# Two graph layers on one core: transposes of the parked batches, and their loads, spread over two steps

## The chip, the cores and the metric

The kernel runs on one core of a Trainium2 chip. The metric is device time in microseconds (us), lower is better. Engines: PE (TensorE, matrix products), DVE (VectorE, elementwise work and 32x32 transposes), ACT (ScalarE, sigmoid, tanh, ReLU and copies out of PSUM), POOL (GpSimd, a few small powers), and SP (SyncE), whose queue issues every DMA of this kernel. Each engine takes its instructions strictly in the order in which they were written.

## The reference

There are 16 batches of 1024 nodes with 128 features, and one dense 1024 x 1024 matrix `adj`. All is float32.

```
h = relu(layernorm(x));  x1 = x + (adj @ (h @ W) + bias)          # layer 0
h = relu(layernorm(x1))                                           # layer 1
repeat 5 times:                                                   # a gated graph step
    m = adj @ h                                                   # in_matrix and out_matrix are both adj
    z = sigmoid(m @ (W3a+W3b) + h @ U3 + biases)
    r = sigmoid(m @ (W4a+W4b) + h @ U3 + biases)
    v = tanh(m @ (W5a+W5b) + (r*h) @ U5 + biases)
    h = (1-z)*h + z*v
out = x1 + h
```

## The kernel before

**Steps.** The batches are worked in four quads of four: quad 0 is batches 0 to 3, quad 1 is 4 to 7, and so on. A step is written (quad, n), n from 0 to 4, and has two stretches. In the *aggregation* `adj @ h` is computed for the quad, with Strassen's scheme at two levels (`aggregate`, 49 small products of four PE records each, about 0.86 us a product). In the *gates* (`gates`, 34.3 us on PE) the small weights are applied, first for pair A (batches 0 and 1 of the quad), then for pair B (batches 2 and 3). A pair has four units (batch, half); its phases are r (four units), z (four) and v (four). Two quads are in work at once, and their steps alternate: (0,0), (1,0), (0,1), [layer 0 of quad 2], (1,1), (0,2), (1,2), (0,3), (1,3), [layer 0 of quad 3], (0,4), (1,4), (2,0), (3,0), (2,1), and so on to (3,4).

**Right operands.** Of the 49 products, 40 take their right operand from `ring` (12 slots). Two operands make one load of 512 KB (`ring<-rd`), issued when a slot has been used; 20 loads for an aggregation. Five of them are issued in the gates before, or at their end (`GATE_LOADS`).

**Left operands** come from `nat`, four loads for each batch (`nat<-fn`, `nat<-ft`), and are added up by DVE and copied by ACT into `big` and `little`, partly in the gates before (`GATE_PLACES`). Among the first of an aggregation are `big[2]` at place 1 and the sums behind it.

**Places.** All side work is hung on places by `put(k, piece)`: place k, a number, is reached after k products of the aggregation; a place with a name is in the gates: `Ar0` comes after the r phase's first unit of pair A, `Az1` after the z phase's second, `Br0` and `Bz1` the same in pair B. At a place the pieces come in the order in which they were put. A place sets where an instruction stands in its engine's queue, SP's included.

**State.** The hidden state stands transposed in `hT_all` (two sets of four batches; quads 0 and 2 use set 0, quads 1 and 3 set 1). After a batch's new state is made, DVE turns it into squares (`sq`, line 669), and SP stores these (`fn<-sq`).

**Norms and parked batches.** In the gates of a step named in `NORMS` DVE takes the statistics of two batches (line 332: four and four `bn_stats` around Ar3 and Az1 for the first, Br3 and Bz1 for the second). In the aggregation of the next step DVE makes their `nmr` (line 349, place 10), and ACT makes the normalized, rectified batch (line 362, from place 11 on). It is *parked*: four stores `ft<-hb` at place 22 for the first and 36 for the second, each followed by a store of x1 (`x1d<-xt`). Before a quad's first step each of its parked batches is loaded (`sqt<-ft`, 512 KB, function `transposing`) and turned into `hT_all` by two DVE transposes of 128 x 512 (line 701).

**Buffers that matter.** `flip` has three buffers for `sq`, `sqt`, `hb`, `ha` and `ho` together. `hv`, which ACT's tanh writes (line 837) and DVE's three update operations use up (lines 238, 839, 241), has three, so that a pair's fourth tanh writes the buffer of its first. An aggregation's PSUM banks are emptied by ACT copies (line 523), and the product that goes on in a bank waits for the copy before.

**Where the turns stand before.** `TRANSPOSED` names the step and the quad: quad 1 in (1,0), quad 2 in (1,4), quad 3 in (3,0). All four loads of a quad stand at places 8, 18, 28 and 38 of that step's aggregation, their turns at 17, 27, 37 and 47. Quad 0's turns are in layer 0 and not touched.

Of the kernel before, what the change touches and what calls it, by code (L numbers as in the profile page):

```python
# [87 lines left out]
    (0, 2): ((12, 26), (13, "Ar1")),  # L88
    (1, 2): ((14, 26), (15, "Ar1")),
}  # L90
TRANSPOSED = {(1, 0): 1, (1, 4): 2, (3, 0): 3}
OUTPUTS = {(3, 0): 0, (2, 1): 1, (3, 1): 2, (2, 2): 3, (3, 2): 4, (2, 3): 5, (3, 3): 6, (2, 4): 7}
UNITS = ((0, 0), (0, 1), (1, 0), (1, 1))

# [2 lines left out]
def tile_two_gnn_layers(  # L97
# [17 lines left out]
    Q = 4  # L115
# [12 lines left out]
    def dma(out, in_):  # L128
        pin(nc.sync.dma_start(out=out, in_=in_))
# [4 lines left out]
    def x_tile(b):  # L134
        return pre.tile([P, NC, D], F32, tag="xt", name=f"xt_{b}")

    def load_x(b, xt=None, parts=((0, NC),)):
        xt = xt if xt is not None else x_tile(b)
        for cs in parts:
            cs = slice(*cs)  # L140
            dma(xt[:, cs], by_slots(x[b])[:, cs])
        return xt
# [14 lines left out]
    hT_all = const.tile([P, 2, Q, N], F32, tag="hT", name="hT_all")  # L157
# [274 lines left out]
    def early_pieces(n):  # L432
        bigs, smalls = left_pieces(n)
        return bigs[0] + smalls[0] + bigs[1] + bigs[3] + smalls[1][:2]

    def period(i):
        return 2 + 7 * i
# [217 lines left out]
    def flip_tile(nm):  # L655
        return flip.tile([P, NSQ, NC, SQ], F32, tag="sq", name=nm)

    def squares_of_half(sq, g):
        return sq[:, :, bass.ts(g, CH), :].rearrange("p k j e -> p j k e")

    def transposed_half(hT, g):
        return hT[:, bass.ts(g, HALF)].rearrange("p (j k e) -> p j k e", j=CH, k=NSQ)
# [28 lines left out]
    def transposing(b, hT):  # L691

        box = {}

        def load():
            box["sq"] = flip_tile(f"sqt_{b}")
            dma(box["sq"].rearrange("p k j e -> p (k j e)"), parked[b][0])

        def turn():
            for g in range(NH):  # L700
                pin(nc.vector.transpose(transposed_half(hT, g), squares_of_half(box["sq"], g)))

        return load, turn
# [4 lines left out]
    def put(k, *pieces):  # L708
        fixed.setdefault(k, []).extend(pieces)
# [56 lines left out]
    def put_statistics(kind, first):  # L766

        rest = []
        for n, b in enumerate((first, first + 1)):
            box = {}  # L770

            def begin(b=b, box=box):
                box["n"] = Norm(xts[b], None, f"{kind}{b}")
                box["n"].statistics(range(CH))

            def relu(k, b=b, box=box):
                def run():
                    if k == 0:
                        box["n"].dst = flip_tile(f"h{kind}_{b}")
                    box["n"].relu(range(2 * k, 2 * k + 2))  # L780

                return run

            def done(b=b, box=box):
                (keep if kind == "a" else layer_1_input)(b, box["n"].dst)

            key = "AB"[n]
            put(f"{key}r3", begin)
            put(f"{key}z1", lambda box=box: box["n"].statistics(range(CH, NC)))
            put(f"{key}z3", lambda box=box: box["n"].scales(EVERY))  # L790
            rest.append((10, lambda box=box: box["n"].shift(EVERY)))
            rest += [(11 + 13 * n + 3 * k, relu(k)) for k in range(CH)]
            rest.append((22 + 14 * n, done))
            if kind == "a":
                rest.append((("Ar0", "Br0")[n], lambda b=b: bias(b)))
        return rest
# [181 lines left out]
    def loads_of_next(source, places):  # L978

        for k, at in enumerate(places):  # L980
            put(at, lambda k=k: natural_from(source[k], nat[:, k]))

    def step(i, loads_at=(period(4), period(5), "Ar0", "Ar2"), early_places=GATE_PLACES):
        st = state[i]
        quad, n = st["quad"], st["step"]
        nm = f"{quad}_{n}"
        hT = [hT_all[:, i, k] for k in range(Q)]
        last = n == STEPS - 1
        final = last and quad == quads - 1
        other = state[1 - i]  # L990
        me = (quad, n)
        for k, piece in relus.pop("next", ()):
            put(k, piece)
        for b, k in LOADS.get(me, ()):
            put(k, lambda b=b: xts.update({b: load_x(b)}))
        if me in TRANSPOSED:
            q = TRANSPOSED[me]
            for k in range(Q):
                load, turn_it = transposing(q * Q + k, hT_all[:, q % 2, k])
                put(8 + 10 * k, load)  # L1000
                put(17 + 10 * k, turn_it)
        if me in OUTPUTS:
            for k, piece in zip((16, 34, 38), outputs[OUTPUTS[me]]):
                put(k, piece)
        block = BLOCKS.get(me)

        source = h0_of(block) if block else other["blocks"]
        if final:
            st["x1"] = []

            def load_x1(k):
                x1 = x_tile(f"1_{quad * Q + k}")
                dma(x1, x1s[quad * Q + k])
                st["x1"].append(x1)

            for k, places in enumerate(((None, 10, 13), (12, 24, 27), (26, 39, 41), (37, "R10", "R11"))):
                for piece, at in zip(outputs[(quad - 1) * Q + k], places):
                    if at is not None:
                        put(at, piece)
            for k, at in enumerate(("R00", "R01", "Z01", "V10")):  # L1020
                put(at, lambda k=k: load_x1(k))
        if source is not None:
            loads_of_next(source, loads_at)
        aggregate(nm, place)
        if me in NORMS:
            relus["next"] = put_statistics(*NORMS[me])
        if source is not None:
            for k, piece in zip(early_places, early_pieces(made[0])):
                put(k, piece)
        stored, ready = {}, {}  # L1030

        def turn(first):
            def run(k):
                k += first
                stored[k] = Later(lambda n: ready[k][n])

                def squares():
                    store, ready[k] = squares_to_dram(hT[k], f"{nm}_{k}")
                    if k >= Q - 2:
                        put({Q - 2: 4, Q - 1: 9}[k], store)  # L1040
                    else:
                        store()

                if k == Q - 1:
                    put(3, squares)
                else:
                    squares()

            return run

        if last:
            outputs.update({quad * Q + k: output(quad * Q + k, Later(lambda n, k=k: ready[k][n])) for k in range(Q)})
            if quad == quads - 2:
                put("Bz1", outputs[quad * Q][0])
        if final:
            last_gates(quad, hT, st["x1"])
            st["quad"], st["blocks"] = None, None
            return
        for a, key in enumerate("AB"):
            pair = slice(2 * a, 2 * a + 2)  # L1060
            gates(
                [mT[:, 2 * a + k] for k in range(2)],
                hT[pair],
                f"{nm}{key}",
                key,
                turn(2 * a),
            )
        st["step"] += 1
        st["blocks"] = [stored[k] for k in range(Q)]
        if last:  # L1070
            begin(i, quad + 2)
        if block:
            loads_of_next(other["blocks"], (period(3) + 4, period(4) + 4, period(5) + 2, period(6)))
            pieces = early_pieces(made[0] + 1)
            for k, piece in zip(BLOCK_PLACES, pieces):
                put(k, piece)
            aggregate(f"a{block}", place, gates_follow=False)
            for k in range(Q):
                for g in range(NH):
                    po(block * Q + k, g)  # L1080
                    if 2 * k + g in (1, 2, 6, 7):
                        pieces[{1: 6, 2: 7, 6: 8, 7: 9}[2 * k + g]]()
            for piece in pieces[10:]:
                piece()
# [4 lines left out]
    def begin(i, quad):  # L1089

        if quad >= quads:
            state[i] = {"quad": None, "blocks": None}
            return
        state[i] = {"quad": quad, "step": 0, "blocks": parked_of(quad)}
# [13 lines left out]
    def h0_of(quad):  # L1108
        return Later(lambda k: h0_blocks[quad * Q + k])
# [108 lines left out]
    for k in range(Q):  # L1218
        b = Q + k
# [56 lines left out]
```

## Time and profile before

| | us |
|---|---|
| median of 3 runs | 1774.37 (1773.52 to 1776.88) |
| profiled execution | 1779.16 |
| its span | 1777.4 |
| PE busy / DVE busy / ACT busy | 1761.9 / 1372.8 / 903.7 |
| gates of (0,0) | 170 to 204 |
| aggregation, gates of (1,0) | 204 to 247, 247 to 281 |
| aggregation, gates of (1,4) | 920 to 963, 963 to 997 |
| aggregation, gates of (2,0) | 997 to 1040, 1040 to 1074 |
| aggregation, gates of (3,0) | 1074 to 1119, 1119 to 1153 |

The span runs from the first to the last of the program's own instructions; around it lie 1.8 us. In rows of instruction groups the numbers are busy time, mean of one in ns, idle time of the engine before them. In rows of the timeline they are start and duration in us, and in brackets the engine's idle time before and what ended it. In lists of waits they are total, times, longest. Names of tiles are shown without the quad: `r_0A` is the r of step 0, pair A, of any quad.

### The profile page before, as it was taken

To read this page: it belongs to the slowest core of one execution; us is meant where nothing else is said; L and a number is where in the kernel's file an instruction comes from. 1 tells how busy PE (TensorE), PEld (TensorE's weight loads), DVE (VectorE), ACT (ScalarE), POOL (GpSimd) and SP (SyncE) were. 2 spreads that over 40 slices of the span, in tenths; PEclk is the share of its full clock that TensorE was granted. 3 is DMA by queue.
4 is the path that set the end of the run, shared out by engine and by line. 5 is a ranking of instruction groups with operands and counts; after the bars stand their busy time and mean duration, and the time that the engine had idled before them with its cause. 6 is when DMAs were issued, how large, how long until landed. Compare 5 with 4: busy or idle time off the path is not lost.

```text
span 1777.4 us, 21433 instructions
## 1 busy us (share of the span) xinstructions
PE 1761.9 (99%) x6438; PEld 1200.4 (68%) x6438; DVE 1372.8 (77%) x2806; ACT 903.7 (51%) x1974; POOL 59.3 (3%) x41
## 2 busy tenths in 40 slices
PE   9999999999999999999999999999999999999998
PEld 3557667588586675858857667585776857667584
DVE  6778988776879687877687968777687777867787
ACT  5246556544555555554455554545445454445544
POOL 3101000000000000000000000000000000000000
PEclk9999999999999999999999999999999999999999
DMA  7489786688395856749839578694866849476794
GB/s 257 158 310 308 235 250 215 176 253 252 123 310 181 267 198 192 241 133 282 263 132 312 185 222 255 168 292 157 250 205 198 253 131 307 153 234 219 195 291 171
DMA packets 169970, 396.88 MB, mean 223 GB/s; under 512 B 18560, under 2 KB 88064, under 8 KB 169856
## 3 DMA queue, kind: packets, MB, share of 16 engines
q1 hardware_dynamic: 169856, 395.52, 70.8%
q8 instruction: 52, 0.85, 0.2%
q14 instruction: 62, 0.51, 0.1%
HBM read 314.44 MB, written 81.00 MB: 222 GB/s over the span
## 4 chain that ended last, share of the span: by engine, by line
PE 89%; DMA 5%; DVE 4%; ACT 1%; POOL 1%; issue 0%; SPq 0%; DVEq 0%; POOLq 0%
PE a L504 25%; PE c L504 12%; PE b L504 6%; PE a_a L504 3%; DMA ring<-rd 3%; PE pr_3B L808 2%; PE pr_1B L808 2%; PE pr_0B L808 2%; PE pr_2B L808 2%; PE pr_2A L808 2%; PE pr_1A L808 2%; PE pr_0A L808 2%; PE pr_3A L808 2%; PE a_a L620 2%; PE pv_0B L808 2%; PE pv_3B L808 2%
## 5 line engine op out<-in xcount | busy, mean ns | idle before, releaser
L504 PE MATMUL a<-ring,big 128*128 128x256 f32 x1120 | 288.3, 380 | 4.4 <-DMA ring<-rd 3.7
L523 ACT COPY Z<-a 128x256 f32<-128x256 f32 x480 | 177.2, 371 | 198.9 <-PE a L504 198.6
L241 DVE TENSOR_TENSOR Z<-Z,taps 128x512 f32<-128x512 f32 (+1 forms) x264 | 144.5, 554 | 167.2 <-ACT taps L523 166.9
L504 PE MATMUL c<-ring,little 128*128 128x256 f32 x960 | 246.6, 379 | 1.2 <-DMA ring<-rd 1.1
L504 PEld LDWEIGHTS a<-ring,big 128*128 128x128 f32 x1120 | 211.7, 190 | 43.5 <-issue 10.5
L241 DVE TENSOR_TENSOR mT<-mT,Z 128x1024 f32<-128x1024 f32 x154 | 188.3, 1223 | 27.4 <-ACT Z L523 22.3
L504 PEld LDWEIGHTS c<-ring,little 128*128 128x128 f32 x960 | 182.0, 190 | 26.9 <-ACT Z L523 1.5
L523 ACT COPY taps<-c 128x256 f32<-128x256 f32 x280 | 103.6, 370 | 117.2 <-PE c L504 112.5
L504 PE MATMUL b<-ring,big 128*128 128x256 f32 x560 | 143.8, 379 | 1.0 <-DMA ring<-rd 1.0
L504 PE MATMUL a<-resident,little 128*128 128x256 f32 x560 | 143.8, 379 | 0.0
L504 PE MATMUL a<-ring,little 128*128 128x256 f32 x560 | 143.7, 379 | 0.0
L504 PEld LDWEIGHTS b<-ring,big 128*128 128x128 f32 x560 | 106.3, 190 | 15.8 <-DMA ring<-rd 1.4
L504 PEld LDWEIGHTS a<-resident,little 128*128 128x128 f32 x560 | 106.3, 190 | 14.7 <-ACT Z L523 0.3
L504 PEld LDWEIGHTS a<-ring,little 128*128 128x128 f32 x560 | 106.4, 190 | 14.5
L669 DVE STREAM_TRANSPOSE sq<-hT_all 128x512 f32<-128x512 f32 x152 | 98.6, 687 | 0.0
L523 ACT COPY taps<-b 128x256 f32<-128x256 f32 x140 | 52.0, 372 | 56.7 <-PE b L504 55.8
L401 ACT COPY big<-nat 128x512 f32<-128x512 f32 x132 | 80.6, 614 | 0.1
L238 DVE TENSOR_TENSOR little<-little,big 128x256 f32<-128x256 f32 x154 | 65.4, 425 | 6.7
L238 DVE TENSOR_TENSOR little<-big 128x256 f32<-128x256 f32 x154 | 64.3, 418 | 0.0
L238 DVE TENSOR_TENSOR little<-big,little 128x256 f32<-128x256 f32 x154 | 64.2, 417 | 0.0
L241 DVE TENSOR_TENSOR little<-big 128x256 f32<-128x256 f32 x154 | 64.0, 416 | 0.2
L523 ACT COPY mT<-a 128x256 f32<-128x256 f32 x80 | 29.8, 372 | 48.1 <-PE a L504 48.0
(282 smaller groups left out, 2912.6 us busy)
## 6 DMA issues: line engine op xcount, KB each, us to landing
ring<-rd SPq DMA_DIRECT2D x440, 512.0 KB, 6.3
fn<-sq SPq DMA_DIRECT2D x76, 512.0 KB, 3.7
nat<-fn SPq DMA_DIRECT2D x256, 128.0 KB, 6.6
x1d<-xt SPq DMA_DIRECT2D x16, 512.0 KB, 5.9
sqt<-ft SPq DMA_DIRECT2D x16, 512.0 KB, 6.8
xt<-x1d SPq DMA_DIRECT2D x16, 512.0 KB, 7.6
xt<-in_x_dram SPq DMA_DIRECT2D x15, 512.0 KB, 6.2
out_dram<-xt SPq DMA_DIRECT2D x14, 512.0 KB, 7.9
```

The costliest lines, as they stand in the source:

```text
L238: pin(nc.vector.tensor_sub(o, a, b))
L241: pin(nc.vector.tensor_add(o, a, b))
L401: return [lambda i=i: pin(nc.scalar.copy(made_of(k, i), part(a, b, i))) for i in range(2)]
L504: nc.tensor.matmul(bank, l, right[:, c, :], start=opens and c == 0, stop=c == SB - 1, skip_group_check=True,)
L523: pin(nc.scalar.copy(to, bank))
L620: nc.tensor.matmul(bank, left[:, c, :], right[c // SB][:, c % SB], start=p in (1, 2, 5) and c == 0, stop=c == CH - 1, skip_group_check=True,)
L669: pin(nc.vector.transpose(squares_of_half(sq, g), transposed_half(hT, g)))
L808: nc.tensor.matmul(bank, w_sb[:, w, :], moving, start=start, stop=stop, skip_group_check=True)
```

## The change

`TRANSPOSED` now lists single batches, each with the place of its load and of its turn. No instruction is added or removed.

```diff
-TRANSPOSED = {(1, 0): 1, (1, 4): 2, (3, 0): 3}
+TRANSPOSED = {
+    (0, 0): ((4, "Ar0", "Az1"), (5, "Br0", "Bz1")),
+    (1, 0): ((6, 8, 17), (7, 28, 34)),
+    (1, 4): ((8, 8, 17), (9, 25, 34), (10, "Ar0", "Az1"), (11, "Br0", "Bz1")),
+    (2, 0): ((12, 8, 17), (13, 25, 34), (14, "Ar0", "Az1"), (15, "Br0", "Bz1")),
+}
...
-        if me in TRANSPOSED:
-            q = TRANSPOSED[me]
-            for k in range(Q):
-                load, turn_it = transposing(q * Q + k, hT_all[:, q % 2, k])
-                put(8 + 10 * k, load)
-                put(17 + 10 * k, turn_it)
+        for b, load_at, turn_at in TRANSPOSED.get(me, ()):
+            load, turn_it = transposing(b, hT_all[:, b // Q % 2, b % Q])
+            put(load_at, load)
+            put(turn_at, turn_it)
```

Quad 1's first two batches move from the aggregation of (1,0) to the gates of (0,0), its last two stay there at places 8 and 28. Of quad 2 two stay in the aggregation of (1,4), two move into that step's gates. All of quad 3 moves from (3,0) to the step before, (2,0): two into its aggregation, two into its gates. On SP the load of batch 4 comes to stand behind the x load of batch 11 and ahead of the third and fourth group of `nat` loads; that of batch 5 behind the store of batch 1's squares; those of batches 10 and 14 behind the second group of `nat` loads; those of 11 and 15 behind the store of their step's second batch. On DVE the turn at Az1 stands among the statistics or early sums of pair A, the turn at Bz1 among those of pair B, ahead of the updates of that pair. Line numbers of the changed kernel are 5 higher behind the table, and 3 higher behind the loop.

## The prediction

> **What bounds the kernel now.** I read the page first, then the list of waits, then single stretches of the timeline.
>
> ```profile
> PE 1761.9 (99%) x6438; PEld 1200.4 (68%) x6438; DVE 1372.8 (77%) x2806; ACT 903.7 (51%) x1974; POOL 59.3 (3%) x41
> ```
>
> PE is busy for 1761.9 of 1777.4 us at a granted clock of 0.999, and the change neither adds nor removes a matmul. All that it can move is PE's idle time, 15.5 us, and new idle time. PE's waits over the whole span:
>
> ```profile
> PE a L504 <- DMA ring<-rd: 3.7, 5, 2.0
> PE c L504 <- DMA ring<-rd: 1.1, 1, 1.1
> PE b L504 <- DMA ring<-rd: 1.0, 1, 1.0
> PE a L504 <- ACT Z L523: 0.7, 3, 0.3
> ```
>
> 5.8 us go to late ring loads. Asked step by step, only two of the steps touched have any. Aggregation (3,0), 1074 to 1119 us, has the first two lines below (1.8 us); aggregation (1,4), 920 to 963, the third.
>
> ```profile
> PE c L504 <- DMA ring<-rd: 1.1, 1, 1.1
> PE a L504 <- DMA ring<-rd: 0.7, 1, 0.7
> ...
> PE a L504 <- DMA ring<-rd: 0.4, 1, 0.4
> ```
>
> The last line of the whole list, "ACT Z", is small but matters most. One of its three waits is at the head of (1,0). ACT there:
>
> ```profile
> 213.92 0.37 ACT L523 COPY taps<-c 128x256 f32<-128x256 f32 x1 [0.49 <-PE c L504]
> 215.74 0.88 ACT L362 ACTIVATE ha<-xt,nmr_a,rstd_a 128x128 f32<-128x128 f32 x2 [1.45 <-DVE nmr_a L349]
> 216.53 0.62 ACT L523 COPY Z<-a 128x256 f32<-128x256 f32 x2
> ```
>
> ACT stands behind nmr of DVE, and the bank copies behind it end at 217.15; the matmul that waits for them starts at 217.20, 0.03 us late. So in a step whose predecessor made statistics ((1,0) after (0,0), (2,0) after (1,4)), DVE has no room at all at the head of the aggregation: lateness that it carries there is PE's. And DVE carries it, since it isn't idle in the second half of such gates.
>
> **The change, part by part.** Sixteen loads (sqt, 512 KB) and sixteen double transposes stay sixteen; twelve of each are concerned. A double transpose holds DVE 1.23 us (967.77 to the next operation at 969.00).
>
> *Taken from aggregations.* (1,0) loses two of its four loads and turns, (1,4) two, (3,0) all four; (2,0) gains two. In (3,0) 4 x 512 KB leave a stretch where the DMA share is 0.96, so its 1.8 us of ring waits should go: -1.8. In (1,4) two loads leave ahead of the late one: -0.4. (1,0) and (2,0) have no ring wait to lose. Two more loads in (2,0) (share 0.87) could cost up to 2 x 1.25 us if all of it were late (1.25 us is 512 KB at the 415 GB/s of a full queue). But (1,4), with the same parking and four such loads, waits 0.4, so two cost 0 to 0.4; I take 0, as PE comes there later anyway (below). DVE's shorter aggregations gain nothing, as no PE wait names those turns.
>
> *Put into the gates of (0,0).* The load of batch 4 goes to Ar0, on SP's queue behind the last x load, and its turn to Az1. DVE and SP there now:
>
> ```profile
> 178.29 1.64 DVE L332 BATCH_NORM_STATS2 stats_a<-xt 128x6 f32<-128x128 f32 x8
> 179.84 0.62 DVE L341 BATCH_NORM_AGGREGATE mv_a<-stats_a 128x2 f32<-128x6 f32 x8
> ...
> 182.82 0.69 DVE L238 TENSOR_TENSOR hv_0A<-hv_0A,hT_all 128x512 f32<-128x512 f32 x1 [2.15 <-ACT hv_0A L837]
> ```
>
> ```profile
> 175.18 0.35 SPq L129 DMA_DIRECT2D xt<-in_x_dram  x1
> 175.88 2.88 SPq L129 DMA_DIRECT2D nat<-ft  x4
> ```
>
> The turn stands after four of the eight statistics (179.05). 2.15 us of idle follow, so it is free if the load lands by 182.82 - 1.60 (the work still to do) - 1.23 = 180.0. But SP issues it only at about 175.9, after the x load, which takes 7.6 us (lands 182.8), because the queues are full from 160 to 192 us. 512 KB at that stretch's 255 to 394 GB/s are 1.3 to 2.1 us, so it lands at 184.1 to 184.9; I take 184.4. DVE is then 4.4 us late. [...] A lone ring load at 206.14 took 3.3 us[...]; here four small loads issued at 175.9 to 178.5 took 6.5 to 7.6, and the row decides.
>
> Queued behind the turn on DVE are the updates of pair A, the squares and r*h of pair B, which PE needs at 198.21 and now has at 194.38: 4.4 us late makes PE wait about 0.6. The rest stays. At Bz1 the turn of batch 5 follows: its load goes out behind the store of batch 1's squares, about 4.2 us before it lands (the ring load at 194.25 took 4.2), just in time for DVE's place (198.95 + 4.4 against 203.0). Another 1.23:
>
> ```profile
> 201.87 0.68 DVE L238 TENSOR_TENSOR hv_0B<-hv_0B,hT_all 128x512 f32<-128x512 f32 x1
> ...
> 203.38 0.69 DVE L241 TENSOR_TENSOR hT_all<-hT_all,hv_0B 128x512 f32<-128x512 f32 x1
> ```
>
> The sum 203.38 + 0.69 + 5.6 = 209.7 frees the hv buffer (three of them) that ACT's fourth tanh, at 204.42 now, writes. ACT is in order, so the copy of the first bank, at 205.28 now, comes about 210.5, and the matmul that needs it (206.81) waits near 4; the nmr chain takes the remainder. With no room in that chain, **the whole 4.4 + 1.2 = 5.6 us reach PE**. Bounds: 1.2 (the load in time, only the Bz1 turn uncovered) to 6.2 (landing 184.9).
>
> *Put into the gates of (1,4).* They start better than now:
>
> ```profile
> 967.77 1.30 DVE L701 STREAM_TRANSPOSE hT_all<-sqt 128x512 f32<-128x512 f32 x2 [6.75 <-DMA sqt<-ft]
> ```
>
> This wait goes: the last two loads move behind it, and Ar0's load, ahead of which SP has two loads less, lands before Az1. What the gates then cost I take from (0,4), which has the same statistics and no turns: 0.69 us idle before hv of pair A, so the Az1 turn leaves 1.23 - 0.69 = 0.54. At Bz1 DVE arrives at 912.93 + 0.54 = 913.5 on that clock; the store before the load goes out at 909.29 + 0.54, the load 0.4 later, 4.2 to land: 914.4. It waits 1.0, then turns 1.23: 2.8 late at pair B's first update. Now (1,4) is there 1.96 late ((994.96 - 962.65) - (915.85 - 885.50)), because of the 6.75. Net +0.85 at the head of (2,0), which has no room. Bounds 0 (load in time) to 2.5 (both turns wholly uncovered).
>
> *Put into the gates of (2,0).* No statistics there, idle 2.99 us before pair A's update and 1.81 before B's: both turns are covered, a late landing included (about 1.4 us late at worst, and (3,0) has no nmr chain). Without that cover 1.2 each.
>
> *Ring loads in the gates* come 1.25 us later behind each moved load. They are used over 17 us after they land. Moved past on SP they cost nothing.
>
> **Sum** against the profiled span: 5.6 + 0.85 - 0.4 - 1.8 = +4.3, 1777.4 to 1781.7 us. That execution took 1779.16 in all, 4.8 more than the median 1774.37 of the plain runs; about that much of ring waits may be the profiler's own, so plain runs may lack both the -2.2 and a part of the backlog behind the +5.6. The two errors oppose each other. On the median: 1778.7.
>
> **Rivals.**
> - *The cover holds* (not slower). One mechanism: the load of batch 4 lands by 180.0. [...] Then (0,0) costs 1.2, (1,4) about 0: 1.2 - 2.2 = -1.0, 1773.4 us. It decides from a landing below about 182, where the sum falls under 3.5 us.
> - *Half cover.* It lands near 182: 2.0 + 1.2 + 0.85 - 2.2 = +1.9, 1776.3.
> - *Ring waits grow in (2,0).* Both added loads fall into a full queue: 4.3 + 2.5 = 6.8, 1781.2. Against it: the 0.4 of (1,4) with four.
> - *No effect:* all moved work is hidden, ring waits are only the profiler's: 1774.4. The idle 2.15 and 2.99 us speak for it, the ACT row at 215.74 against it.
> - *Faster:* it would take the 3.3 us of ring waits in untouched steps to go too, 1774.4 - 5.5 = 1768.9. Nothing in the profile links them.
>
> **How the numbers follow.** Main case 0.53 (own range 1777 to 1780.7, the landing's bounds), ring waits grow 0.10, half cover 0.13, cover holds 0.12, no effect 0.07, faster 0.05. A change within 0.2% (3.5 us) can't be told from none. Of the main case about a tenth lies below 1777.9, so slower is 0.48 + 0.10 + a few hundredths of half cover = 0.62; same is 0.31, faster 0.07. The range, 1773.0 to 1781.6, leaves out "faster" and the tails.
>
> **What would show it.** Right: in the gates of (0,0) a DVE transpose with about 5 us idle before it, released by the sqt load; ACT's fourth tanh of pair B released by DVE; a PE wait of some 4 us at the head of (1,0); no ring wait in (3,0). Wrong: that transpose starts by 180 us, or PE doesn't wait at the head of (1,0); or ring waits appear at the end of (2,0).

## The result and the profile after

The changed kernel takes 1780.38 us (median of 5 runs, 1778.8 to 1782.6), the kernel before 1774.33 beside it. The ratio of matched runs is 1.0026, 95% interval 1.0014 to 1.0038: slower by some 4.6 us (2.5 to 6.7). That figure comes from runs paired in time; the two medians alone lie 6.05 us apart. The prediction was +4.3 us.

The two profiled executions can't be set against each other as totals: the one of before took 1779.16 us, more than its median, and the one of after 1778.80. Only their stretches can be compared. PE's work on the page of after is what it was:

```profile
PE 1762.0 (99%) x6438; PEld 1201.8 (68%) x6438; DVE 1373.8 (77%) x2806; ACT 903.4 (51%) x1974; POOL 59.3 (3%) x41
```

PE's list of waits over the span of after (total, times, longest):

```profile
PE a L509 <- ACT mT L528: 3.1, 1, 3.1
...
PE a L509 <- ACT Z L528: 1.3, 2, 1.0
PE a L509 <- DMA ring<-rd: 1.3, 1, 1.3
```

The first line is new and is the head of aggregation (1,0). Of the second, 1.0 us is the head of (2,0). The ring waits of (1,4) and (3,0) are gone, and the one that is left lies near 600 us, in a step that the change does not touch.

**DVE in the gates of (0,0)**, timeline of after (start, duration, in brackets the idle time before and what ended it):

```profile
178.19 0.87 DVE L337 BATCH_NORM_STATS2 stats_a<-xt 128x6 f32<-128x128 f32 x4
183.77 1.31 DVE L706 STREAM_TRANSPOSE hT_all<-sqt 128x512 f32<-128x512 f32 x2 [4.71 <-DMA sqt<-ft]
...
186.48 0.68 DVE L243 TENSOR_TENSOR hv_0A<-hv_0A,hT_all 128x512 f32<-128x512 f32 x1
...
202.63 1.30 DVE L706 STREAM_TRANSPOSE hT_all<-sqt 128x512 f32<-128x512 f32 x2
...
206.75 0.68 DVE L243 TENSOR_TENSOR hv_0B<-hv_0B,hT_all 128x512 f32<-128x512 f32 x1
```

The load of batch 4 was issued at 175.3 and landed 8.4 us later. DVE waits 4.71 us for it after half of the statistics and is 3.66 us late at pair A's first update (182.82 before). The second turn needs no wait, takes its 1.2 us, and pair B's first update starts at 206.75 instead of 201.87. PE's matmuls ahead of this stretch start 0.10 us earlier than in before (the start-up of the two executions), so DVE is **4.98 us late**.

**ACT behind it**, same stretch of after:

```profile
209.04 0.69 ACT L842 ACTIVATE hv_0B<-pv_0B,bsum 128x512 f32<-128x512 f32 x1 [5.67 <-DVE hT_all L246]
209.63 0.36 ACT L528 COPY mT<-a 128x256 f32<-128x256 f32 x1
...
220.61 0.88 ACT L367 ACTIVATE ha<-xt,nmr_a,rstd_a 128x128 f32<-128x128 f32 x2 [1.36 <-DVE nmr_a L354]
```

In before, the same tanh and the copy of the first bank:

```profile
204.42 0.69 ACT L837 ACTIVATE hv_0B<-pv_0B,bsum 128x512 f32<-128x512 f32 x1 [1.03 <-PE pv_0B L808]
205.28 0.37 ACT L523 COPY mT<-a 128x256 f32<-128x256 f32 x1 [0.17 <-PE a L504]
```

In after the fourth tanh waits 5.67 us for DVE to give a buffer back, and the first bank's copy stands behind it: 209.63 against 205.28. ACT's 1974 instructions come in the same order in both traces, and so do PE's 6438. **PE**, in before and then in after:

```profile
206.81 1.03 PE L504 MATMUL a<-ring,little 128*128 128x256 f32 x4
```

```profile
205.93 1.03 PE L509 MATMUL c<-ring,little 128*128 128x256 f32 x4
210.04 2.07 PE L509 MATMUL a<-ring,little 128*128 128x256 f32 x4 [3.09 <-ACT mT L528]
211.91 1.75 PE L509 MATMUL a<-ring,big 128*128 128x256 f32 x4
213.50 1.03 PE L509 MATMUL c<-ring,little 128*128 128x256 f32 x4
```

A group of four takes 1.03 us elsewhere; the two behind the wait take 2.07 and 1.75. Stretches of after with the granted clock behind POOL's column:

```profile
206.55:209.96 3.41, 0.41 (x2) 0.00 (x1) 3.20 (x8) 0.92 (x3) 1.92 (x1) 1.00 0.48 154
209.96:213.37 3.41, 3.33 (x8) 2.67 (x9) 3.27 (x6) 0.95 (x4) 0.00 (x0) 0.50 0.14 19
```

After 3.41 us in which PE was busy for 0.41, the next 3.41 us ran at half clock. To see what each step costs, I followed every matmul's start in both traces and took the difference. From 190 us to the end of this head it grows by 4.97 us, DVE's lateness again: 0.08 at r*h of pair B, 3.25 at the wait, 1.64 over the matmuls at half clock. ACT's wait for nmr, 1.36 us (1.45 before), adds nothing: PE is by then as late as DVE.

**The other steps of after.** DVE in the gates of (1,4), then of (2,0):

```profile
975.63 1.30 DVE L706 STREAM_TRANSPOSE hT_all<-sqt 128x512 f32<-128x512 f32 x2
...
994.82 1.30 DVE L706 STREAM_TRANSPOSE hT_all<-sqt 128x512 f32<-128x512 f32 x2 [1.41 <-DMA sqt<-ft]
...
1056.65 0.69 DVE L243 TENSOR_TENSOR hv_0A<-hv_0A,hT_all 128x512 f32<-128x512 f32 x1 [1.81 <-ACT hv_0A L842]
```

The turn at Az1 of (1,4) is in time, the one at Bz1 waits 1.41 us, and the head of (2,0) loses 1.28 us behind nmr. In (2,0) DVE is still idle for 1.81 us behind its first turn, so that one is covered. The second turn waits 2.17 us for its load, at 1072.79, and makes DVE 1.56 us late at pair B's first update (1075.38 against 1069.85, PE being 3.97 us late already); yet PE loses nothing at the head of (3,0). In (1,4) and (3,0) PE gains 0.67 and 2.60 us in matmul starts against the profiled execution of before, whose ring waits are gone.

### The profile page after: what moved, and what is told of

Its sections match the earlier page's. It is cut to its first block, busy times and chain, and to the rows that moved or that the text cites. A ratio compares the mean times of both kernels' runs of the same rounds, so it can differ in the third digit from the quotient of the medians.

```text
span 1777.0 us, 21432 instructions
## 1 busy us (share of the span) xinstructions
PE 1762.0 (99%) x6438; PEld 1201.8 (68%) x6438; DVE 1373.8 (77%) x2806; ACT 903.4 (51%) x1974; POOL 59.3 (3%) x41
## 4 chain that ended last, share of the span: by engine, by line
PE 89%; DMA 5%; DVE 4%; POOL 1%; ACT 1%; issue 1%; SPq 0%; DVEq 0%; POOLq 0%; ACTq 0%
PE a L509 26%; PE c L509 13%; PE b L509 6%; PE a_a L509 3%; PE pr_1B L813 2%; PE pr_3B L813 2%; PE pr_2A L813 2%; PE pr_3A L813 2%; PE pr_2B L813 2%; PE pr_1A L813 2%; DMA ring<-rd 2%; PE pr_0B L813 2%; PE pr_0A L813 2%; PE a_a L625 2%; PE pv_2A L813 2%; PE pv_3A L813 2%
```

## The experiments

Each kernel ran in five rounds beside the kernel before (median there 1776.0 to 1776.9 us), and was profiled once. 0.001 of ratio is 1.8 us. "Loss" is how much the difference of PE's matmul starts against the trace of before grows, for (1,0) from 190 to 235 us, for (2,0) from 990 to 1025, by before's clock. Before itself has small waits in the second, so that a loss of -0.46 is none. The losses are those of one execution each, and some of these are among the fastest of their kernel (load later: 1779.32 us, median 1783.33); the ratios are those of all. (1,4) and (3,0), where ring waits come off, are not in the two columns.

| edit | ratio [95%] | loss at (1,0) | loss at (2,0) |
|---|---|---|---|
| the change | 1.0026 [1.0014, 1.0038] | 4.97 | 1.28 |
| quad 1 alone | 1.0025 [1.0014, 1.0036] | 3.97 | -0.46 |
| quads 2 and 3 alone | 1.0003 [0.9992, 1.0013] | 0.01 | 1.28 |
| load of batch 4 early | 1.0010 [1.0000, 1.0020] | 1.45 | 1.30 |
| load of batch 4 later | 1.0038 [1.0023, 1.0053] | 6.95 | 1.39 |
| load early, nmr and ReLU later | 1.0009 [1.0001, 1.0017] | 1.38 | 1.92 |
| load early, only ReLU later | 0.9994 [0.9984, 1.0003] | -0.09 | -0.12 |
| no turns at Bz1 in (0,0), (1,4) | 0.9997 [0.9989, 1.0006] | 0.01 | -0.46 |
| the same, nmr and ReLU later | 0.9993 [0.9983, 1.0004] | 0.16 | -0.46 |
| before, nmr and ReLU later | 1.0005 [0.9996, 1.0014] | 0.16 | 0.48 |
| quad 3 alone | 1.0008 [0.9996, 1.0020] | 0.01 | 0.19 |
| change, four hv buffers | 1.0045 [1.0029, 1.0062] | 8.21 | 1.28 |
| change, four hv buffers, ReLU later | 1.0025 [1.0017, 1.0032] | 2.05 | 0.06 |

### Which quad, and is it the load?

In the first four runs theory A puts the loss on DVE's lateness in the gates of (0,0), of which batch 4's load makes most. B gives the moved work a price of its own, whenever that load lands. C puts the loss on quads 2 and 3.

Quad 1 alone:

```diff
     (0, 0): ((4, "Ar0", "Az1"), (5, "Br0", "Bz1")),
     (1, 0): ((6, 8, 17), (7, 28, 34)),
-    (1, 4): ((8, 8, 17), (9, 25, 34), (10, "Ar0", "Az1"), (11, "Br0", "Bz1")),
-    (2, 0): ((12, 8, 17), (13, 25, 34), (14, "Ar0", "Az1"), (15, "Br0", "Bz1")),
+    (1, 4): ((8, 8, 17), (9, 18, 27), (10, 28, 37), (11, 38, 47)),
+    (3, 0): ((12, 8, 17), (13, 18, 27), (14, 28, 37), (15, 38, 47)),
```

> Only quad 1 is spread as in the change (batches 4 and 5 in the gates of (0,0)); quads 2 and 3 stand as before. Theory A (the late load of batch 4 makes DVE late in the gates of (0,0), and PE pays all of that at the head of (1,0)): about +4.9 us against before, 1779.2; in the trace the transpose of batch 4 waits over 4 us for its load, and PE stops about 3 us and then runs at half clock at the head of (1,0). Rival B (every turn put into gates costs alike, six of them): a third of the loss, about +2, 1776.3. Rival C (the loss sits in ring waits of steps that the change doesn't touch): 0, 1774.3.

Measured: 1.0025, +4.4 us. Quads 2 and 3 alone:

```diff
-    (0, 0): ((4, "Ar0", "Az1"), (5, "Br0", "Bz1")),
-    (1, 0): ((6, 8, 17), (7, 28, 34)),
+    (1, 0): ((4, 8, 17), (5, 18, 27), (6, 28, 37), (7, 38, 47)),
```

> Quad 1 stands as before, quads 2 and 3 are spread as in the change. Theory A: +0.8 at the head of (2,0), and the ring waits of (1,4) and (3,0) go, which are 2.2 us in a profile and perhaps less in a plain run: 1772.9 to 1775.1. Rival B (every turn in gates costs alike): two thirds of the loss, about +4, 1778.3. Rival C: as the change, 1780.

Measured: 1.0003, +0.5 us. The two add up to 4.9 us, the change is 4.6, and their intervals don't overlap: quad 1 is most of the change's cost, and C falls. DVE and PE with quad 1 alone:

```profile
183.11 1.31 DVE L706 STREAM_TRANSPOSE hT_all<-sqt 128x512 f32<-128x512 f32 x2 [3.74 <-DMA sqt<-ft]
...
209.35 1.13 PE L509 MATMUL a<-ring,little 128*128 128x256 f32 x4 [2.16 <-ACT mT L528]
```

Here the load came a little sooner, PE's first wait is 2.16 us instead of 3.09, and the clock stayed whole (1.00 in each of the nine us from 205 to 214). So part of the loss comes later in the head: 1.18 of the 3.97 us behind nmr, and 0.35 at a product whose left operand is a late sum of DVE (more on it below).

The load of batch 4, and nothing else, issued in the aggregation before:

```diff
-    (0, 0): ((4, "Ar0", "Az1"), (5, "Br0", "Bz1")),
+    (0, 0): ((4, 42, "Az1"), (5, "Br0", "Bz1")),
```

> The change with one edit: the load of batch 4 is issued at place 42 of the aggregation of (0,0), ahead of the last parked batch and of two x loads, and its turn stays at Az1. It should land near 173 us. Theory A: the turn no longer waits, fits into DVE's idle time before pair A's update, and only the Bz1 turn's 1.2 us reach PE: about 3.7 less than the change, 1776.7 (1775.4 to 1777.5), and no half clock at the head of (1,0). Rival B (the turns' own DVE work or the transfers in the gates cost, not the landing): as the change, 1780.4.

Measured: 1.0010, 2.8 us less than the change; A had said 3.7, with a range of 2.9 to 5.0. The same load at a later place:

```diff
-    (0, 0): ((4, "Ar0", "Az1"), (5, "Br0", "Bz1")),
+    (0, 0): ((4, "Ar1", "Az1"), (5, "Br0", "Bz1")),
```

> The change with one edit: the load of batch 4 is issued at Ar1, behind four nat loads, so it lands about 2.2 us later. Theory A: DVE waits about 7 instead of 4.7 us, and PE pays each us of it: +2.2 against the change, 1782.6. Rival B: as the change, 1780.4.

Measured: 1.0038, 2.1 us more than the change (A: 2.2). The interval of either run overlaps that of the change; the two runs, with the same work moved and only this load's place between them, are 5.0 us apart, and their intervals do not overlap. With DVE's wait for the load at 0, 3.74, 4.71 and 6.54 us in these traces, PE lost 1.45, 3.97, 4.97 and 6.95. Between the waits of 3.74 and 6.54, 2.8 apart, the losses are 3.0 apart: one for one. **B falls.** With the later load even r*h of pair B is late, which it wasn't in the change (its list of waits):

```profile
PE a L509 <- ACT mT L528: 3.2, 1, 3.2
...
PE pv_0B L813 <- DVE r_0B L826: 1.6, 1, 1.6
```

### What is left with the load early

The load being early, DVE, ACT and PE of that run:

```profile
199.36 1.30 DVE L706 STREAM_TRANSPOSE hT_all<-sqt 128x512 f32<-128x512 f32 x2 [0.17 <-DMA sqt<-ft]
203.47 0.68 DVE L243 TENSOR_TENSOR hv_0B<-hv_0B,hT_all 128x512 f32<-128x512 f32 x1
```

```profile
205.77 0.69 ACT L842 ACTIVATE hv_0B<-pv_0B,bsum 128x512 f32<-128x512 f32 x1 [2.22 <-DVE hT_all L246]
217.35 0.88 ACT L367 ACTIVATE ha<-xt,nmr_a,rstd_a 128x128 f32<-128x128 f32 x2 [2.90 <-DVE nmr_a L354]
```

```profile
218.81 1.13 PE L509 MATMUL a<-ring,big 128*128 128x256 f32 x4 [1.05 <-ACT Z L528]
```

The turn at Bz1 makes DVE late: 203.47 against 201.87, less 0.16 by which this execution was later all along, is 1.44 us. The late tanh no longer delays PE. The copies behind the ReLU that waits for nmr do, for 1.19 us, and the product with a late sum, at 213.94, and the one behind it had lost the other 0.26 before. Two ways to test it. First, nmr on DVE and the ReLU pieces on ACT four places later:

```diff
-            rest.append((10, lambda box=box: box["n"].shift(EVERY)))
-            rest += [(11 + 13 * n + 3 * k, relu(k)) for k in range(CH)]
+            rest.append((14, lambda box=box: box["n"].shift(EVERY)))
+            rest += [(15 + 9 * n + 2 * k, relu(k)) for k in range(CH)]
```

> The kernel with batch 4's load early, and with nmr moved from place 10 to 14 and the ReLU pieces to places 15, 17, 19, 21 and 24, 26, 28, 30. Theory N (what is left of the loss reaches PE through the nmr and ReLU chain at the head of the next aggregation, ahead of which stand the bank copies on ACT): the loss at the head of (1,0) falls from 1.6 us to at most 0.4 and that of (2,0) from 1.2 to at most 0.4, so the time is some 2 us below the kernel with the early load, ratio to before about 0.9999. Rival M (it reaches PE through DVE's other work there, the sums of left operands, or through ACT's late copies themselves): both losses stay, ratio about 1.0010.

Measured: 1.0009, and both losses stay. Taken alone that speaks for M. But the trace shows why it could not tell:

```profile
219.17 0.69 DVE L246 TENSOR_TENSOR Z<-Z,taps 128x512 f32<-128x512 f32 x1
219.77 0.24 DVE L354 SCALAR_TENSOR_TENSOR nmr_a<-mv_a,rstd_a 128x8 f32<-128x8 f32 x2
```

```profile
219.97 0.88 ACT L367 ACTIVATE ha<-xt,nmr_a,rstd_a 128x128 f32<-128x128 f32 x2 [2.19 <-DVE nmr_a L354]
```

nmr now stands behind the sums of four more places, and DVE, which is busy without a break here, reaches it 2.6 us later than in the run before (217.15). ACT's ReLU still waits 2.19 us. So a later run moved the ReLU pieces alone and left nmr at place 10:

```diff
-            rest += [(11 + 13 * n + 3 * k, relu(k)) for k in range(CH)]
+            rest += [(15 + 9 * n + 2 * k, relu(k)) for k in range(CH)]
```

> Batch 4's load early; nmr stays at place 10 on DVE, and only the ReLU pieces on ACT go to places 15, 17, 19, 21 and 24, 26, 28, 30. With nmr moved too, nmr came 2.5 us later behind more of DVE's work, so that run did not open the chain. Theory N (the rest of the loss reaches PE because the bank copies stand on ACT behind a ReLU that waits for DVE's nmr): the losses at the heads of (1,0) and (2,0), 1.6 and 1.2 us with the early load alone, fall to at most 0.4 each; ratio 0.9997 to 1.0003. Rival M (DVE's other work there, the sums of left operands, carries it): both stay, ratio about 1.0010.

Measured: 0.9994, 2.8 us less than with the load early alone, a little beyond what N said (the two intervals just overlap, so the trace has to decide). ACT there:

```profile
217.62 0.37 ACT L528 COPY taps<-b 128x256 f32<-128x256 f32 x1 [0.49 <-PE b L509]
217.88 0.88 ACT L367 ACTIVATE ha<-xt,nmr_a,rstd_a 128x128 f32<-128x128 f32 x2
```

The ReLU finds nmr done, no copy is late, and PE has no wait at either head. DVE is still late, 1.18 us at pair B's first update against 1.44 (203.30, start-up 0.25): **N holds** for the greater part, for (1,0) and (2,0) alike. The 0.26 at the late sum is gone too; it goes with a lateness that is now within that sum's room (1.4, below).

Second, no turn at Bz1 in gates with statistics; batch 5, and 8 to 10, turned in aggregations:

```diff
+    (0, 0): ((4, 42, "Az1"),),
+    (1, 0): ((5, 8, 17), (6, 18, 27), (7, 28, 37)),
+    (1, 4): ((8, 8, 17), (9, 18, 27), (10, 28, 37), (11, "Ar0", "Az1")),
```

> Turns only where DVE is idle: in gates with statistics (those of (0,0) and (1,4)) one turn at Az1 with its load issued early (batch 4 at place 42, batch 11 at Ar0), none at Bz1; batches 5, 6, 7 in the aggregation of (1,0) at places 8, 18, 28 and 8, 9, 10 in that of (1,4); quad 3 as in the change. Theory A (the loss is made by the wait for batch 4's load and by the turns at Bz1): heads of (1,0) and (2,0) within 0.3 us of before, ring waits of (3,0) gone; -0.3 to -2.5 us, ratio 0.9986 to 0.9998. Rival B (moving loads and turns costs by their number, wherever they stand): +1 us or more, ratio 1.0005 or above.

Measured: 0.9997, -0.5 us (-2.0 to +1.1), and in the trace no wait of PE at either head, or in (1,4) and (3,0). The ReLU at the head of (1,0) waits what it waited before (1.45 us there):

```profile
215.51 0.88 ACT L367 ACTIVATE ha<-xt,nmr_a,rstd_a 128x128 f32<-128x128 f32 x2 [1.46 <-DVE nmr_a L354]
```

A holds, at the weak end of what it said for the time. With nmr and ReLU later besides (the diff of the first test on this kernel):

> The former kernel (no turns at Bz1) with nmr and ReLU 4 places later. Theory N: adds up to 0.5 us to that kernel's gain (the nmr chain had 0.2 to 0.3 us of wait at each of four heads), ratio 0.9982 to 0.9998. Rival: the later ReLU pieces push the parking stores into the ring loads, and it is 0.5 us or more above that kernel.

Measured: 0.9993, which can't be told from the run before or from the kernel before. The control, that edit alone on the kernel before:

> The kernel before with nmr and ReLU 4 places later, nothing else. Theory N: only the three waits of 0.3 us behind ACT's bank copies go, -0.3 to -0.7 us, ratio 0.9996 to 0.9999: the late nmr helps only where DVE is late. Rival: a gain of 2 us or as much as in the kernel with the early load, so that the later nmr says nothing of the change.

Measured: 1.0005, no gain; the trace even loses 0.48 us at the head of (2,0). With nmr and ReLU moved together, then, none of three kernels was shown to gain. The edit that did gain, the ReLU pieces alone, was not run on the kernel before, so how much of its 2.8 us that kernel would gain too is open; in the traces the two heads account for 3.0 us (1.45 + 1.30 against -0.09 and -0.12).

### The ring waits of (3,0)

Quad 3 alone as in the change, quads 1 and 2 as before:

```diff
-    (3, 0): ((12, 8, 17), (13, 18, 27), (14, 28, 37), (15, 38, 47)),
+    (2, 0): ((12, 8, 17), (13, 25, 34), (14, "Ar0", "Az1"), (15, "Br0", "Bz1")),
```

> Only quad 3's part of the change: its four loads and turns leave the aggregation of (3,0) for (2,0) and its gates; quads 1 and 2 as before. Theory A (ring waits of (3,0) go, gates of (2,0) cover the turns): no new wait in (2,0) or at the head of (3,0), two ring waits of (3,0) gone, 1.8 us in the profile, less in plain runs: ratio 0.9990 to 0.9999. Rival: two more loads in the aggregation of (2,0) make ring waits there, or the turns in its gates reach the head of (3,0): ratio 1.0003 or more.

Measured: 1.0008, interval 0.9996 to 1.0020. The trace does what A said: the ring waits of (3,0) are gone, nothing is lost at its head, and (2,0) shows 0.2 us of ring wait. Yet the time shows no gain; by its ratio alone it would be the rival's run (1.0003 or more), and its trace is of the fastest of its 14 runs (1772.84 us, median 1776.77), so what the slower ones lost is not shown. A likely reason for the missing gain is in two other traces, in which quad 3 stands as before; PE's ring waits in (3,0), in the run with quad 1 alone and in the control with later nmr:

```profile
PE c L509 <- DMA ring<-rd: 0.7, 1, 0.7
```

```profile
PE c L508 <- DMA ring<-rd: 0.2, 1, 0.2
```

The profiled execution of before had 1.8 on its list, and in matmul starts it lost 2.60 us there against the change; these two lost 0.97 and 0.41. If that is usual, so much and not 2.6 was to be gained in the plain runs, too little for these runs to resolve.

### Which chain carries DVE's lateness

The changed kernel with a fourth hv buffer, so that the fourth tanh need not wait for DVE:

```diff
-            hv = work.tile([P, HALF], F32, tag="hv", name=f"hv_{tag}", bufs=3)
+            hv = work.tile([P, HALF], F32, tag="hv", name=f"hv_{tag}", bufs=4)
```

(and the same number at the two other tiles with that tag).

> The changed kernel with a fourth hv buffer, so that the fourth tanh of pair B need not wait for DVE's updates. Theory A (two chains carry DVE's lateness, and each alone is enough): the wait of some 3.1 us for the first bank at the head of (1,0) goes, and a wait of 4 to 5 us behind nmr takes its place, with or without a stretch at half clock behind it; loss at the head of (1,0) 4.5 to 6.5 us, ratio about 1.0026. Rival T (only the hv buffer passes it on): loss at most 1.6 us, ratio 1.0007 or below.

Measured: 1.0045. T falls: no bank copy is late, and PE loses no less. Why it takes longer than with three buffers is not shown beyond this trace (the intervals overlap), and four buffers were not run on the kernel before. In this execution the load of batch 4 landed later still; DVE, then PE:

```profile
186.77 1.30 DVE L706 STREAM_TRANSPOSE hT_all<-sqt 128x512 f32<-128x512 f32 x2 [7.60 <-DMA sqt<-ft]
```

```profile
201.09 2.07 PE L813 MATMUL pv_0B<-r_0B,w_sb 128*128 128x512 f32 x2 [2.71 <-DVE r_0B L826]
...
220.25 1.20 PE L509 MATMUL a<-ring,big 128*128 128x256 f32 x4 [1.93 <-issue]
```

4.42 us are lost at r*h and 3.79 at a product of the head, both with a stretch at half clock (0.50 from 200.64 and from 221.12). A had expected the second wait behind nmr, and it isn't there; the profile names no releaser for it. The fourth buffer with the ReLU pieces later as well:

> The changed kernel with a fourth hv buffer and the ReLU pieces 4 places later (nmr stays at place 10): both chains loosened, DVE as late as in the change. Theory A: the loss at the head of (1,0) falls from 4.9 to 1.5 us or less, since 4 places are 3.4 us, and that of (2,0) to at most 0.4; ratio 1.0000 to 1.0010. Rival M (DVE's sums of left operands carry the lateness to PE by themselves): loss 3 us or more, ratio 1.0018 or more.

Measured: 1.0025; the trace lost 2.05 us at (1,0), at the same product (DVE, then PE):

```profile
214.98 1.29 DVE L243 TENSOR_TENSOR big<-big,nat 128x512 f32<-128x512 f32 x2
```

```profile
215.77 1.10 PE L509 MATMUL a<-ring,big 128*128 128x256 f32 x4 [1.79 <-issue]
```

The load was waited for 3.10 us here. The sum `big` in before:

```profile
211.54 1.29 DVE L238 TENSOR_TENSOR big<-big,nat 128x512 f32<-128x512 f32 x2
```

It is 3.44 us late, 3.34 without the start-up. Its first half ends at 215.66, and the product starts 0.1 us after. No releaser is named, but the times of all fourteen traces agree: in four of them (quad 1 alone, load early, both runs with four buffers) the product starts 0.1 us after this half, and in no trace sooner. In before 1.48 us lie between the two, so the sum has a room of 1.4 us. A, which allowed a loss of 1.5 us and a ratio of 1.0010, falls; M is nearer: DVE's sums carry the lateness, less their room. The 2.05 us of this trace don't account for the whole time, though: it is of the second fastest of 22 runs (1776.55 us, median 1780.16), and what the others lose is not shown.

So at the head of (1,0) three chains hang on DVE: the hv buffer with the tanh (a lateness of 1.44 passed with no loss; 3.96 with quad 1 alone cost 2.43, 4.98 in the change 3.25), the left operands' sums (room of 1.4), and nmr with the ReLU ahead of the bank copies (none). Which of them PE meets depends on how late DVE is and on which are loosened.

## Why the prediction was right

The sum of the parts was +4.3 and the ratio gives +4.6. The path was right: the late load, DVE's lateness carried to the head of (1,0), PE's wait there. That the two numbers lie as close as 0.3 us is in part luck: the cost at (1,0) was put 0.6 us too high and that at (2,0) 0.4 too low, and the gain from ring waits, by the traces below, 0.9 to 1.8 too high. By its steps:

- *Load of batch 4: landing at 184.4, 4.4 us late.* It landed at 183.7 in the profiled run, and pair A was 3.7 late. The step held, a little too high, and of the two times weighed there those of the row were the nearer: 8.4 us from issue to landing, against 6.5 to 7.6 of the small loads and 3.3 of the lone ring load. But the landing is not one number. Four kernels with the same order on SP up to that load made DVE wait 3.10, 3.74, 4.71 and 7.60 us.
- *Turn at Bz1: 1.2, its load just in time.* Right: no wait, 1.2 added, 4.98 late in all.
- *r*h of pair B: PE waits about 0.6.* The wait in after was under 0.1, since pair A was 3.7 late and not 4.4. It appears with more lateness: 1.6 us at a DVE wait of 6.54, 2.7 at 7.60.
- *The whole 5.6 reaches PE at the head of (1,0).* 4.98 were there at DVE, and 4.97 reached PE: the step held at the smaller size. The way was partly another. The wait behind the tanh was 3.25 (near 4 predicted), and the rest, which nmr was to add, came from the clock: 1.64 us at half speed, a term that the prediction did not have. It probably cost nothing on top, since the other chains would have held PE for about as long. Where the wait was shorter and the clock stayed whole (quad 1 alone) nmr did add 1.18 as written, and the operand sums, a chain that the prediction did not name, 0.35.
- *(1,4) to the head of (2,0): +0.85.* 1.28: the load of batch 11 was waited for 1.41 us, where 1.0 was reckoned.
- *Gates of (2,0): covered; ring waits in (2,0): 0.* Right; DVE was 1.56 us late there (1.4 at worst, it said), at no cost to PE. The 415 GB/s behind the 1.25 us of a load is a rate that before reached only in places: 416 from 164 to 166 us at a DMA share of 1.03, but 244 from 180 to 182 at 1.13.
- *Ring waits: -0.4 and -1.8.* The mis-sized term. The profiled pair shows -0.67 and -2.60 in matmul starts, but with quads 2 and 3 as before two other executions had only 0.4 and 1.0 us to gain in (3,0), and 0 and 0.4 in (1,4); moving quad 3 alone gained nothing measurable. The prediction feared this and set it against a lower backlog behind the +5.6. The plain runs don't show that backlog gone: with the load late they are 5.0 us above those with the load early. A slip on the way: the list of waits has eight lines, not the four shown, and the ring waits of untouched steps come to 3.5 us, not 3.3; neither enters the +4.3.

In the traces the two heads cost 4.97 + 1.28 = 6.25 us, and if the ring waits that come off in (1,4) and (3,0) are the 0.4 to 1.3 us of those two executions, 4.9 to 5.8 are left, inside the measured 2.5 to 6.7. The rival *cover holds* priced its landing about rightly: with the load early the trace has 1.45 at (1,0) where it had 1.2. But it had that load come early by itself. No version here was shown to beat the kernel before; the lowest ratios, 0.9993 and 0.9994, have intervals that reach over 1.

## What to carry to other kernels

Here a transpose of 1.2 us was moved to where its engine had 2 us idle, and nearly all that it cost was the lateness of its operand's load and the next turn behind it. That load took 8.4 us from issue while the DMA engines were busy throughout (a share of 1.08 from 175.3 to 183.8 us of after); a lone one, the ring load at 206.14 of before, took 3.3 (a share of 0.00 in the 2 us up to 206). Before moving such work, look at when its load can be issued and what is in flight then. Follow everything that stands behind it on its engine to the next place where the bottleneck engine has no room, and list all chains between the two with the room of each: here there were three. A gain that is read from small waits of one profiled execution should be looked for in a second execution before it enters a sum.

## What the runs showed of the hardware

**Half clock after a wait that is shorter than others which had none.** PE idle for 3.09 and 3.22 us (the change, the later load) was followed by 3.41 us at a granted clock of 0.50, and so were idle times of 2.71 and only 1.93 us with four hv buffers; behind idle times of 2.61 (load early, only ReLU later, near 1721 us), 2.16 (quad 1 alone) and 1.79 us (four hv buffers, ReLU later) the clock stayed at 1.00. Stretches of the run with four hv buffers (PE's busy time after the length; the clock behind POOL's column):

```profile
197.23:200.64 3.41, 1.16 (x3) 0.19 (x1) 3.27 (x6) 0.85 (x2) 0.00 (x0) 1.00 0.01 4
200.64:204.05 3.41, 2.96 (x4) 1.41 (x5) 3.38 (x9) 0.69 (x1) 0.00 (x0) 0.50 0.86 282
217.71:221.12 3.41, 1.48 (x7) 0.87 (x5) 3.27 (x7) 0.52 (x2) 0.00 (x0) 1.00 1.00 341
221.12:224.53 3.41, 3.41 (x10) 2.70 (x9) 3.31 (x10) 0.88 (x3) 0.00 (x0) 0.50 0.62 247
```

The clock falls at 200.64, while PE is still idle, and at 221.12, when it has been at work again for 0.9 us; each time it is 0.50 for the 3.41 us that follow. In before an idle time of 1.96 us, about as long as the 1.93, left it whole:

```profile
598.99:602.40 3.41, 1.45 (x8) 1.30 (x8) 1.29 (x2) 0.66 (x2) 0.00 (x0) 1.00 1.05 389
602.40:605.81 3.41, 3.41 (x17) 2.81 (x16) 1.87 (x3) 1.39 (x5) 0.00 (x0) 1.00 0.83 267
```

So the length of the idle time doesn't sort these cases. Nor does PE's busy time in the stretch around it: ahead of the fall at 221.12 it was 1.48 us of 3.41; here it is 1.45, and with the load early and only the ReLU later 0.40 of the 3 us from 1720, and the clock did not fall. What decides was not shown; no run varied it on purpose. A wait of the same length may thus cost 1.7 us more (an estimate, half of 3.41 us at a clock of 0.50; 1.64 was measured in the change) or nothing.
